# Projection and second norm cut into pieces, with their transposes between groups of qkv columns

## The chip, the cores and the metric

The kernel runs on one core of one Trainium2 chip. The metric is device time in microseconds of one execution; the time before is the median of three runs. Everything is fp32.

## The reference, cut to what matters

The input is x of 8 batches x 512 tokens x 576 features. First a rotation in a 64-dimensional subspace is applied per batch. Then one transformer block follows, with "attention" over the 16 heads of each token itself:

```
z = x @ U;  x = x + (z @ R - z) @ U.T                    # U from a QR, R = expm(skew(cond))
s1, c1, g1, s2, c2, g2 = split(silu(cond) @ ada_w + ada_b)
h = layernorm(x) * (1 + c1) + s1
q, k, v = h @ qkv_w + qkv_b                              # per token: 16 heads x 36
a = softmax(q k^T / 6) v                                 # 16 x 16 inside one token
x = x + g1 * (reorder(a) @ proj_w + proj_b)              # heads moved in front of tokens
h2 = layernorm(x) * (1 + c2) + s2
x = x + g2 * (gelu(h2 @ fc1_w + fc1_b) @ fc2_w + fc2_b)
```

The reordering in front of the projection mixes tokens: the attention result goes to device memory (`att_d`) and is read back in another layout (`at`).

## The kernel before, in words

After a preparation (QR, matrix exponential, modulation vectors) the kernel makes 16 passes, hb = 0 to 15. Each covers 256 tokens, two tiles (t = 0, 1) of 128; two passes make a batch (b = hb // 2). In pass hb the main loop does, in program order:

- `qkv(hb + 1, 0)`: the qkv product of tile 0 of the next pass. Its 1,728 columns are cut into four groups of 432; each group is five products over the feature chunks (`qkvp`, L631), one bank of PSUM, and a ScalarE copy to `qkv` (L638).
- `project(hb)`: for each tile, five transposes of `at` in two banks (`atr`, L702), two ScalarE copies to `aT` (L703), and two halves of the projection (`pj`, L709), which VectorE multiplies by the gate (`pt`, L711) and adds to `x1` (L712).
- `qkv(hb + 1, 1)`: the same for tile 1.
- `mlp_input(hb)`: the second layer norm of both tiles on VectorE (`normed`, L542 to L546, with one power on GpSimd, L545), then five pairs of transposes (`h2tr`, L555), each evicted by a ScalarE instruction that applies scale and shift (`h2T`, L558), and a GpSimd addition to `x1` of each tile (L721).
- `mlp(hb)`: 18 tiles f of fc1 (`fc`, L740; gelu on ScalarE, L742), and fc2 two tiles behind (L752). Weights are streamed from device memory through SP's queue in rings of four. In even passes the rotation of the next batch and its first norm (`gps` L577, `zps` L586, `rot` L594, `htr` L555) are put between the tiles of fc1.
- `attention(hb + 1)`: VectorE's products and reductions (`qk` L652, `sc` L658, `pv` L675, `att` L681), which run beside the MLP of pass hb, and the two stores to `att_d`.

The eight PSUM banks are three rings: `ps_mm` with two banks (tag "mm": qkvp, atr, pj, h2tr, and the rotation's products), `ps_f1` with two (tag "f1": fc1 alone), and `ps_acc` with four for fc2. A ring's next tile waits until the tile two before it has been evicted.

A scheduler orders each engine's instructions from the program order, the dependencies and its own durations. On the chip each engine follows its own list in that order. So an instruction late in the program can stand a little ahead of an earlier one that the scheduler believed to be waiting.

Of the kernel before, what the change touches and what calls it, by code (L numbers as in the profile page):

```python
# [9 lines left out]
F32 = mybir.dt.float32  # L10
U32 = mybir.dt.uint32
AF = mybir.ActivationFunctionType
ALU = mybir.AluOpType
# [4 lines left out]
B, S, D = 8, 512, 576  # L18
# [3 lines left out]
NT = S // 128  # L22
KROWS = [128, 128, 128, 128, 64]
NK = len(KROWS)
HALF = D // 2
# [4 lines left out]
TAU, M8 = 16, 8  # L30
# [12 lines left out]
def rotate_then_dit_block(  # L43
# [15 lines left out]
    nc = tc.nc  # L59
# [14 lines left out]
    xr_d = [dram.tile([NT, 128, D], F32, tag=f"xr_{b}", name=f"xr_{b}") for b in range(B)]  # L74
    att_d = [dram.tile([H, S, DH], F32, tag=f"att_{b}", name=f"att_{b}") for b in range(B)]

    ident = const.tile([128, 128], F32, tag="ident", name="ident")
# [9 lines left out]
    mod = const.tile([128, 4, NK, B], F32, tag="mod", name="mod")  # L87
# [3 lines left out]
    wproj = const.tile([128, NK, D], F32, tag="wproj", name="wproj")  # L91

    def srows(c):
        return 65 if c == 4 else 128
# [36 lines left out]
    with tc.manual_schedule(engines=engines), tc.tile_pool(name="prep", bufs=1) as prep, tc.tile_pool(name="qrs", bufs=2) as qrs, tc.tile_pool(  # L131
        name="ada", bufs=10
    ) as adap, tc.tile_pool(name="exs", bufs=1) as exs, tc.tile_pool(
        name="ps_qr", bufs=1, space=PSUM
    ) as ps_qr, tc.tile_pool(name="ps_a", bufs=1, space=PSUM) as ps_a, tc.tile_pool(
        name="ps_ex", bufs=2, space=PSUM
    ) as ps_ex, tc.tile_pool(name="ps_m", bufs=2, space=PSUM) as ps_m:
        m = prep.tile([128, NK, R], F32, tag="m", name="m")
# [260 lines left out]
        t = column_products(0)  # L399
        for j in range(R):  # L400
            t = qr_step(j, t)
# [11 lines left out]
        if True:  # L413
            sq = qrs.tile(wide(R), F32, tag="up0", name="sq", bufs=1)
            nc.vector.tensor_tensor(sq, m, m, ALU.mult)
            t = qrs.tile([128, R], F32, tag="t", name="t_sq")
# [42 lines left out]
            for c, rows in enumerate(KROWS):  # L459
                ps = ps_ex.tile([R, 128], F32, tag="ex", name=f"vt_{c}")  # L460
# [16 lines left out]
            ps = ps_m.tile([R, R], F32, tag="m", name="s_ps")  # L477
# [4 lines left out]
            for c, rows in enumerate(KROWS):  # L482
                ps = ps_m.tile([128, R], F32, tag="m", name=f"u_{c}")
# [5 lines left out]
            for n in range(2):  # L489
                ps = ps_m.tile([128, HALF], F32, tag="m", name=f"ut_{n}")  # L490
                nc.tensor.matmul(
                    ps,
                    lhsT=sneg.rearrange("p h i -> p (h i)"),
                    rhs=vt[:, n * HALF : (n + 1) * HALF],
                    start=True,
                    stop=True,
                )
                nc.scalar.copy(ut[:, n * HALF : (n + 1) * HALF], ps)
            for h in range(2):
                p = slice(h * R, (h + 1) * R)  # L500
# [3 lines left out]
    tiles = ctx.enter_context(tc.tile_pool(name="tiles", bufs=2))  # L504
    small = ctx.enter_context(tc.tile_pool(name="small", bufs=4))
    wst = ctx.enter_context(tc.tile_pool(name="wst", bufs=4))
    ps_mm = ctx.enter_context(tc.tile_pool(name="ps_mm", bufs=2, space=PSUM))
    ps_f1 = ctx.enter_context(tc.tile_pool(name="ps_f1", bufs=2, space=PSUM))
# [13 lines left out]
    ats = padded("at", 2)  # L522
    turn = {"xn": 0, "at": 0}

    def take(which, ring):
        turn[which] += 1
        return ring[(turn[which] - 1) % len(ring)]
# [7 lines left out]
    def normed(xt, name):  # L535

        st = small.tile([128, 2, 6], F32, tag="st", name=f"st_{name}")
        mv = small.tile([128, 2], F32, tag="mv", name=f"mv_{name}")
        rs = small.tile([128, 1], F32, tag="rstd", name=f"rstd_{name}")
        xn = take("xn", xns)  # L540
        for n in range(2):
            nc.vector.bn_stats(st[:, n, :], xt[:, n * HALF : (n + 1) * HALF])  # L542
        nc.vector.bn_aggr(mv, st)
        nc.vector.tensor_scalar(rs, mv[:, 1:2], LN_EPS, None, ALU.add)  # L544
        nc.gpsimd.tensor_tensor(rs, rs, mhalf[:, 0:1], ALU.pow)  # L545
        nc.vector.tensor_scalar(xn[:, 0:D], xt, mv[:, 0:1], rs, ALU.subtract, ALU.mult)  # L546
        return xn

    def modulated(dst_of, pair, shift, b, name):

        for c in range(NK):
            rows = srows(c)
            ps = ps_mm.tile([128, 2, 128], F32, tag="mm", name=f"{name}_{c}")
            for t in range(2):
                nc.tensor.transpose(ps[:, t, :], pair[t][:, c * 128 : (c + 1) * 128], ident)  # L555
            dst, src = dst_of(c, rows, ps[0:rows])
            sh, scl = mod[0:rows, shift, c, b : b + 1], mod[0:rows, shift + 1, c, b : b + 1]
            nc.scalar.activation(dst, src, AF.Identity, bias=sh, scale=scl)  # L558

    hTs = {}  # L560

    normed_x = {}
# [46 lines left out]
    def feature_major(b, half):  # L609

        if half == 0:
            hTs[b] = big.tile([128, NK, S], F32, tag="hT", name=f"hT_{b}")
        hT = hTs[b]

        def in_order(c, rows, ps):
            dst = hT[0:rows, c, :].rearrange("p (h t m) -> p t h m", t=NT, m=M8)[:, 2 * half : 2 * half + 2]
            return dst, ps.rearrange("p t (h m) -> p t h m", m=M8)

        modulated(in_order, normed_x.pop((b, half)), 0, b, f"htr_{b}_{half}")

    def qkv(hb, t):

        b, hT = hb // 2, hTs[hb // 2]
        i = 2 * (hb % 2) + t
        tok = tiles.tile([128, 3 * D], F32, tag="qkv", name=f"qkv_{b}_{i}", bufs=3)
        N = 3 * D // 4
        for n in range(4):
            ps = ps_mm.tile([128, N], F32, tag="mm", name=f"qkvp_{b}_{i}_{n}")
            for c in range(NK):
                k = srows(c)  # L630
                nc.tensor.matmul(  # L631
                    ps,
                    lhsT=hT[0:k, c, i * 128 : (i + 1) * 128],
                    rhs=wqkv[0:k, c, n * N : (n + 1) * N],
                    start=c == 0,
                    stop=c == NK - 1,
                )
            nc.scalar.copy(tok[:, n * N : (n + 1) * N], ps)  # L638
        return tok

    def attention(hb, toks):

# [42 lines left out]

    x1s = {}

    def project(hb, gate):
        b = hb // 2
        pair = []  # L690
        rows = att_d[b].rearrange("h (m t) d -> h m (t d)", t=TAU)
        for t in range(2):
            i = 2 * (hb % 2) + t
            at = take("at", ats)
            nc.sync.dma_start(out=at[:, 0:D], in_=rows[:, i * M8 : (i + 1) * M8, :])
            x1 = tiles.tile([128, D], F32, tag="x1", name=f"x1_{hb}_{t}", bufs=4)
            nc.sync.dma_start(out=x1, in_=xr_d[b][i])
            aT = tiles.tile([128, NK, 128], F32, tag="aT", name=f"aT_{hb}_{t}")
            for c0, c1 in ((0, 4), (4, 5)):
                ps = ps_mm.tile([128, 4, 128], F32, tag="mm", name=f"atr_{hb}_{t}_{c0}")  # L700
                for c in range(c0, c1):
                    nc.tensor.transpose(ps[:, c - c0, :], at[:, c * 128 : (c + 1) * 128], ident)  # L702
                nc.scalar.copy(aT[:, c0:c1, :], ps[:, 0 : c1 - c0, :])  # L703
            for n in range(2):
                cols = slice(n * HALF, (n + 1) * HALF)
                ps = ps_mm.tile([128, HALF], F32, tag="mm", name=f"pj_{hb}_{t}_{n}")
                for c in range(NK):
                    k = srows(c)
                    nc.tensor.matmul(ps, lhsT=aT[0:k, c, :], rhs=wproj[0:k, c, cols], start=c == 0, stop=c == NK - 1)  # L709
                tmp = tiles.tile([128, HALF], F32, tag="tmp", name=f"pt_{hb}_{t}_{n}", bufs=3)  # L710
                nc.vector.tensor_tensor(tmp, ps, gate[:, cols], ALU.mult)  # L711
                nc.vector.tensor_tensor(x1[:, cols], x1[:, cols], tmp, ALU.add)  # L712
            pair.append(x1)
        x1s[hb] = pair

    def mlp_input(hb, gb2):
        pair = [normed(x1, f"m{hb}_{t}") for t, x1 in enumerate(x1s[hb])]
        h2T = tiles.tile([128, NK, 256], F32, tag="h2T", name=f"h2T_{hb}")
        modulated(lambda c, rows, ps: (h2T[0:rows, c, :], ps.rearrange("p t s -> p (t s)")), pair, 2, hb // 2, f"h2tr_{hb}")
        for x1 in x1s[hb]:  # L720
            nc.gpsimd.tensor_tensor(x1, x1, gb2, ALU.add)  # L721
        return h2T

    LAG = 2

# [45 lines left out]
    NH = 2 * B  # L771
# [1 line left out]
        piece()  # L773
    feature_major(0, 0)
    feature_major(0, 1)
    toks = [qkv(0, 0), qkv(0, 1)]
    for v in (2, 3, 4, 5):
        for c in range(NK):
            load_ada(v, c, wst)
# [3 lines left out]
    for hb in range(NH):  # L783
        b = hb // 2
        aside = {}
        if hb % 2 == 0:
            gate_a, gate_m = gate_rows(0, b), gate_rows(1, b)
            gb2 = big.tile([128, D], F32, tag="gb2", name=f"gb2_{b}")
            nc.gpsimd.tensor_tensor(gb2, gate_m, b2, ALU.mult)
        if hb + 1 < NH:  # L790
            toks = [qkv(hb + 1, 0)]
        project(hb, gate_a)
        if hb + 1 < NH:
            toks.append(qkv(hb + 1, 1))
        if hb % 2 == 0 and b + 1 < B:
            aside = dict(zip((1, 3, 4, 6, 7, 8), rotation(b + 1)))
            aside |= {12: lambda: feature_major(b + 1, 0), 15: lambda: feature_major(b + 1, 1)}
        h2T = mlp_input(hb, gb2)
        mlp(hb, h2T, gate_m, aside)
        if hb + 1 < NH:  # L800
            attention(hb + 1, toks)
# [48 lines left out]
```

## Time and profile before

| | us |
|---|---|
| median of three runs (2331.64 to 2333.31) | 2332.75 |
| the profiled execution | 2331.75 |
| its span, first to last instruction | 2329.8 |
| TensorE products, busy | 2205.8 (95%) |
| TensorE weight loads, busy | 1656.0 (71%) |
| VectorE, busy | 1740.9 (75%) |
| ScalarE, busy | 385.3 (17%) |
| GpSimd, busy | 212.7 (9%) |
| DMA queue 1, share of 16 engines | 40.6% |

The mean granted TensorE clock is 0.986. A pass takes some 118 us where it is odd and 131 where it is even and carries the next batch's rotation; the whole of the 16 passes begins near 361 us. Busy time of products is modelled at its end, so it overstates how full TensorE is; the chain of waits tells more. Line numbers in the profile (L631) are those of the kernel printed above.

### The profile page before, as it was taken

To read this page: it belongs to the slowest core of one execution; us is meant where nothing else is said; L and a number is where in the kernel's file an instruction comes from. 1 tells how busy PE (TensorE), PEld (TensorE's weight loads), DVE (VectorE), ACT (ScalarE), POOL (GpSimd) and SP (SyncE) were. 2 spreads that over 40 slices of the span, in tenths; PEclk is the share of its full clock that TensorE was granted. 3 is DMA by queue.
4 is the path that set the end of the run, shared out by engine and by line. 5 is a ranking of instruction groups with operands and counts; after the bars stand their busy time and mean duration, and the time that the engine had idled before them with its cause. 6 is when DMAs were issued, how large, how long until landed. Compare 5 with 4: busy or idle time off the path is not lost.

```text
span 2329.8 us, 25839 instructions
## 1 busy us (share of the span) xinstructions
PE 2205.8 (95%) x9857; PEld 1656.0 (71%) x9857; DVE 1740.9 (75%) x2241; ACT 385.3 (17%) x872; POOL 212.7 (9%) x309
## 2 busy tenths in 40 slices
PE   6779788999999999999999999999999999999998
PEld 5668464767777676868686767777776868686877
DVE  8878399959595969768695959595968788595910
ACT  1012111211121202111111212121211112111110
POOL 2034001100010000010100010000100010101010
PEclk9999978999999999999999999999999999999999
DMA  7000322543536262626263444525262626252543
GB/s 251 1 4 2 115 74 62 162 135 102 143 108 189 60 178 57 201 63 165 69 197 100 126 113 150 147 84 160 95 180 65 171 67 165 75 157 82 152 121 111
DMA packets 206632, 271.41 MB, mean 116 GB/s; under 512 B 84115, under 2 KB 108395, under 8 KB 206510
## 3 DMA queue, kind: packets, MB, share of 16 engines
q1 hardware_dynamic: 206510, 269.77, 40.6%
q8 instruction: 79, 1.29, 0.2%
q14 instruction: 43, 0.35, 0.1%
HBM read 241.23 MB, written 28.35 MB: 116 GB/s over the span
## 4 chain that ended last, share of the span: by engine, by line
PE 89%; DVE 5%; ACT 2%; issue 1%; DMA 1%; POOL 1%; SPq 0%; POOLq 0%; ACTq 0%
PE fc L740 27%; PE fc L752 24%; PE qkvp L631 20%; PE pj L709 6%; PE zps L586 2%; PE dp L227 1%; PE rot L594 1%; PE h2tr L555 1%; PE htr L555 1%; PE aps L277 1%; ACT aT L703 1%; PE rp L219 1%; PE ada L118 1%; DVE up L257 1%; ACT qkv L638 1%
## 5 line engine op out<-in xcount | busy, mean ns | idle before, releaser
L740 PE MATMUL fc<-h2T,w 128*128 128x256 f32 (+1 forms) x2880 | 674.5, 380 | 0.0
L740 PEld LDWEIGHTS fc<-h2T,w 128*128 128x128 f32 (+1 forms) x2880 | 543.0, 191 | 83.2 <-issue 0.4
L752 PE MATMUL fc<-w,gt 128*128 128x288 f32 x2304 | 600.6, 405 | 0.0
L752 PEld LDWEIGHTS fc<-w,gt 128*128 128x128 f32 x2304 | 435.8, 189 | 109.6
L652 DVE TENSOR_TENSOR qk<-qkv 128x2304 f32<-128x2304 f32 x128 | 353.3, 2790 | 173.2 <-ACT qkv L638 173.2
L631 PE MATMUL qkvp<-wqkv,hT 128*128 128x432 f32 (+1 forms) x1280 | 474.6, 530 | 2.2 <-DVE pt L711 2.2
L631 PEld LDWEIGHTS qkvp<-wqkv,hT 128*128 128x128 f32 (+1 forms) x1280 | 244.2, 191 | 219.0 <-issue 212.4
L658 DVE TENSOR_REDUCE sc<-qk 128x64 f32<-128x2304 f32 x128 | 322.5, 2536 | 0.0
L675 DVE TENSOR_TENSOR pv<-sc,qkv 128x2304 f32<-128x2304 f32 x128 | 322.0, 2547 | 0.3
L681 DVE TENSOR_REDUCE att<-pv 128x144 f32<-128x2304 f32 x128 | 321.4, 2544 | 0.2
L764 DVE TENSOR_TENSOR mt<-fc,gate 128x288 f32<-128x288 f32 x64 | 29.3, 458 | 303.0 <-PE fc L752 283.3
L742 ACT ACTIVATE gt<-fc 128x256 f32<-128x256 f32 x288 | 110.4, 383 | 861.3 <-PE fc L740 861.1
L709 PE MATMUL pj<-wproj,aT 128*128 128x288 f32 (+1 forms) x640 | 163.9, 411 | 8.9 <-ACT aT L703 8.8
L638 ACT COPY qkv<-qkvp 128x432 f32<-128x432 f32 x128 | 66.3, 518 | 572.5 <-PE qkvp L631 572.5
L709 PEld LDWEIGHTS pj<-wproj,aT 128*128 128x128 f32 (+1 forms) x640 | 118.9, 190 | 45.6 <-ACT aT L703 15.1
L765 POOL TENSOR_TENSOR x<-x,mt 128x288 f32<-128x288 f32 x64 | 48.8, 795 | 949.3 <-DVE mt L764 949.3
L219 PE MATMUL rp<-m,ident 128*128 128x64 f32 (+42 forms) x128 | 40.7, 409 | 36.4 <-DVE m L265 32.6
L219 PEld LDWEIGHTS rp<-m,ident 128*128 128x128 f32 x128 | 32.0, 311 | 43.4 <-DVE m L265 38.2
L545 POOL TENSOR_TENSOR rstd_m<-rstd_m,mhalf 128x1 f32<-128x1 f32 x32 | 19.7, 616 | 458.9 <-DVE rstd_m L544 458.9
L545 POOL TENSOR_TENSOR rstd_a<-rstd_a,mhalf 128x1 f32<-128x1 f32 x32 | 25.3, 790 | 360.0 <-DVE rstd_a L544 360.0
L227 PE MATMUL dp<-t,ones 128*128 128x64 f32 (+42 forms) x128 | 39.0, 396 | 14.1 <-DVE sgs L235 13.6
L721 POOL TENSOR_TENSOR x<-x,gb 128x576 f32<-128x576 f32 x32 | 47.2, 1476 | 22.2 <-DVE xn L546 22.2
(204 smaller groups left out, 1402.0 us busy)
## 6 DMA issues: line engine op xcount, KB each, us to landing
w<-in_fc_w SPq DMA_DIRECT2D x288, 320.0 KB
w<-in_fc_w SPq DMA_DIRECT2D x288, 288.0 KB
xT<-in_x_t SPq DMA_DIRECT2D x16, 640.0 KB
xt<-in_x SPq DMA_DIRECT2D x32, 288.0 KB
xr<-xt SPq DMA_DIRECT2D x32, 288.0 KB
x<-xr SPq DMA_DIRECT2D x32, 288.0 KB
att<-att SPq DMA_DIRECT2D x32, 288.0 KB
at<-att SPq DMA_DIRECT2D x32, 288.0 KB
```

The costliest lines, as they stand in the source:

```text
L219: nc.tensor.matmul(rp[:, j:R], lhsT=ident[:, j : j + 1].to_broadcast([128, 128]), rhs=m[:, 0, j:R], start=True, stop=True,)
L227: nc.tensor.matmul(dp[:, j:R], lhsT=ones, rhs=t[:, j:R], start=True, stop=True)
L631: nc.tensor.matmul(ps, lhsT=hT[0:k, c, i * 128 : (i + 1) * 128], rhs=wqkv[0:k, c, n * N : (n + 1) * N], start=c == 0, stop=c == NK - 1,)
L638: nc.scalar.copy(tok[:, n * N : (n + 1) * N], ps)
L652: nc.vector.tensor_tensor(pr, q[:, c * HC : (c + 1) * HC].unsqueeze(2).to_broadcast([128, HC, H, DH]), k.unsqueeze(1).to_broadcast([128, H ...
L658: nc.vector.tensor_reduce(sc2[:, t, c * HC : (c + 1) * HC, :], pr, AX.X, ALU.add)
L675: nc.vector.tensor_tensor(pr, sc2[:, t, c * HC : (c + 1) * HC, :].unsqueeze(2).to_broadcast([128, HC, DH, H]), v.unsqueeze(1).to_broadcast ...
L681: nc.vector.tensor_reduce(att[:, c * HC : (c + 1) * HC, :], pr, AX.X, ALU.add)
L709: nc.tensor.matmul(ps, lhsT=aT[0:k, c, :], rhs=wproj[0:k, c, cols], start=c == 0, stop=c == NK - 1)
L740: nc.tensor.matmul(ps, lhsT=w1[0:k, c, :], rhs=h2T[0:k, c, :], start=c == 0, stop=c == NK - 1)
L742: nc.scalar.activation(gs[f], ps, AF.Gelu)
L752: nc.tensor.matmul(acc[t, n], lhsT=gs[f][:, t * 128 : (t + 1) * 128], rhs=w2[:, n * HALF : (n + 1) * HALF], start=f == 0, stop=f == NF - 1,)
```

## The change

`project` and `mlp_input` become a class `Projection` with four methods: `turn(t)` (the five transposes of attention tile t and their copies), `product(t, n)` (one half of the projection), `norm(t)` (the second norm of a tile, and the GpSimd addition to it), and `turn_normed(cs)` (the transposes and evictions of one or two feature chunks). `qkv` returns a function that does one group of columns. The main loop calls the pieces in a new order. The transposes of both kinds take their banks from `ps_f1` in place of `ps_mm`, and the second kind puts two feature chunks into one bank. The first norm's transposes keep their ring; their code is only written out in place. No instruction of arithmetic is added or removed.

```diff
-    def project(hb, gate):
-    def mlp_input(hb, gb2):
...
     def qkv(hb, t):
...
-        for n in range(4):
+        def group(n):
             ps = ps_mm.tile([128, N], F32, tag="mm", name=f"qkvp_{b}_{i}_{n}")
...
-        return tok
+        return tok, group
...
+    class Projection:
+        def __init__(self, hb, gate):
...
+            for t in range(2):
+                i = 2 * (hb % 2) + t
+                at = take("at", ats)
+                nc.sync.dma_start(out=at[:, 0:D], in_=rows[:, i * M8 : (i + 1) * M8, :])
+                x1 = tiles.tile([128, D], F32, tag="x1", name=f"x1_{hb}_{t}", bufs=4)
+                nc.sync.dma_start(out=x1, in_=xr_d[b][i])
...
+        def turn(self, t):
+            aT = tiles.tile([128, NK, 128], F32, tag="aT", name=f"aT_{self.hb}_{t}")
             for c0, c1 in ((0, 4), (4, 5)):
-                ps = ps_mm.tile([128, 4, 128], F32, tag="mm", name=f"atr_{hb}_{t}_{c0}")
+                ps = ps_f1.tile([128, 4, 128], F32, tag="f1", name=f"atr_{self.hb}_{t}_{c0}")
                 for c in range(c0, c1):
-                    nc.tensor.transpose(ps[:, c - c0, :], at[:, c * 128 : (c + 1) * 128], ident)
+                    nc.tensor.transpose(ps[:, c - c0, :], self.at[t][:, c * 128 : (c + 1) * 128], ident)
                 nc.scalar.copy(aT[:, c0:c1, :], ps[:, 0 : c1 - c0, :])
...
+        def product(self, t, n):
+            aT, x1 = self.aT[t], x1s[self.hb][t]
+            cols = slice(n * HALF, (n + 1) * HALF)
+            ps = ps_mm.tile([128, HALF], F32, tag="mm", name=f"pj_{self.hb}_{t}_{n}")
+            for c in range(NK):
+                k = srows(c)
+                nc.tensor.matmul(ps, lhsT=aT[0:k, c, :], rhs=wproj[0:k, c, cols], start=c == 0, stop=c == NK - 1)
+            tmp = tiles.tile([128, HALF], F32, tag="tmp", name=f"pt_{self.hb}_{t}_{n}", bufs=3)
+            nc.vector.tensor_tensor(tmp, ps, self.gate[:, cols], ALU.mult)
+            nc.vector.tensor_tensor(x1[:, cols], x1[:, cols], tmp, ALU.add)
+
+        def norm(self, t, gb2):
+            x1 = x1s[self.hb][t]
+            self.xn.append(normed(x1, f"m{self.hb}_{t}"))
             nc.gpsimd.tensor_tensor(x1, x1, gb2, ALU.add)
+
+        def turn_normed(self, cs):
...
+            ps = ps_f1.tile([128, 2, 2, 128], F32, tag="f1", name=f"h2tr_{self.hb}_{cs[0]}")
+            for k, c in enumerate(cs):
+                for t in range(2):
+                    nc.tensor.transpose(ps[:, k, t, :], self.xn[t][:, c * 128 : (c + 1) * 128], ident)
+            for k, c in enumerate(cs):
+                rows = srows(c)
+                nc.scalar.activation(
+                    self.h2T[0:rows, c, :],
+                    ps[0:rows, k].rearrange("p t s -> p (t s)"),
+                    AF.Identity,
+                    bias=mod[0:rows, 2, c, b : b + 1],
+                    scale=mod[0:rows, 3, c, b : b + 1],
+                )
...
-        if hb + 1 < NH:
-            toks = [qkv(hb + 1, 0)]
-        project(hb, gate_a)
-        if hb + 1 < NH:
-            toks.append(qkv(hb + 1, 1))
+        pr = Projection(hb, gate_a)
+        (tok0, q0), (tok1, q1) = [qkv(hb + 1, t) if hb + 1 < NH else (None, lambda n: None) for t in range(2)]
+        toks = [tok0, tok1]
+        for n in range(3):
+            q0(n)
+        pr.turn(0)
+        q0(3)
+        pr.product(0, 0)
+        pr.turn(1)
+        pr.product(0, 1)
+        pr.norm(0, gb2)
+        pr.product(1, 0)
+        pr.product(1, 1)
+        pr.norm(1, gb2)
+        for n in range(3):
+            q1(n)
+        pr.turn_normed((0, 1))
+        q1(3)
+        pr.turn_normed((2, 3))
+        pr.turn_normed((4,))
+        h2T = pr.h2T
...
-        h2T = mlp_input(hb, gb2)
         mlp(hb, h2T, gate_m, aside)
```

More of the change, by code (lines that the diff above doesn't have):

```diff
@@ L547, in normed @@
         return xn
[L549 to L558, printed above, removed]
     hTs = {}
@@ L613, in feature_major @@
         hT = hTs[b]
[L615 to L619, printed above, removed]
+        pair = normed_x.pop((b, half))
+        for c in range(NK):
+            rows = srows(c)
+            ps = ps_mm.tile([128, 2, 128], F32, tag="mm", name=f"htr_{b}_{half}_{c}")
+            for t in range(2):
+                nc.tensor.transpose(ps[:, t, :], pair[t][:, c * 128 : (c + 1) * 128], ident)
+            nc.scalar.activation(
+                hT[0:rows, c, :].rearrange("p (h t m) -> p t h m", t=NT, m=M8)[:, 2 * half : 2 * half + 2],
+                ps[0:rows].rearrange("p t (h m) -> p t h m", m=M8),
+                AF.Identity,
+                bias=mod[0:rows, 0, c, b : b + 1],
+                scale=mod[0:rows, 1, c, b : b + 1],
+            )
     def qkv(hb, t):
@@ L686, in rotate_then_dit_block @@
     x1s = {}
-    def project(hb, gate):
[L689 to L698, printed above, removed]
+    class Projection:
+        def __init__(self, hb, gate):
+            self.hb, self.gate, b = hb, gate, hb // 2
+            rows = att_d[b].rearrange("h (m t) d -> h m (t d)", t=TAU)
+            self.at, self.aT, self.xn, x1s[hb] = [], [], [], []
+            for t in range(2):
[4 more added lines that the diff above has]
+                nc.sync.dma_start(out=x1, in_=xr_d[b][i])
+                self.at.append(at)
+                x1s[hb].append(x1)
+        def turn(self, t):
+            aT = tiles.tile([128, NK, 128], F32, tag="aT", name=f"aT_{self.hb}_{t}")
@@ L699, in project @@
             for c0, c1 in ((0, 4), (4, 5)):
-                ps = ps_mm.tile([128, 4, 128], F32, tag="mm", name=f"atr_{hb}_{t}_{c0}")
+                ps = ps_f1.tile([128, 4, 128], F32, tag="f1", name=f"atr_{self.hb}_{t}_{c0}")
                 for c in range(c0, c1):
-                    nc.tensor.transpose(ps[:, c - c0, :], at[:, c * 128 : (c + 1) * 128], ident)
+                    nc.tensor.transpose(ps[:, c - c0, :], self.at[t][:, c * 128 : (c + 1) * 128], ident)
                 nc.scalar.copy(aT[:, c0:c1, :], ps[:, 0 : c1 - c0, :])
[L704 to L712, printed above, removed]
@@ L713, in project @@
-            pair.append(x1)
-        x1s[hb] = pair
-    def mlp_input(hb, gb2):
[L717 to L722, printed above, removed]
+            self.aT.append(aT)
+        def product(self, t, n):
+            aT, x1 = self.aT[t], x1s[self.hb][t]
+            cols = slice(n * HALF, (n + 1) * HALF)
+            ps = ps_mm.tile([128, HALF], F32, tag="mm", name=f"pj_{self.hb}_{t}_{n}")
+            for c in range(NK):
+                k = srows(c)
[3 more added lines that the diff above has]
+            nc.vector.tensor_tensor(x1[:, cols], x1[:, cols], tmp, ALU.add)
@@ new lines, in norm @@
+        def norm(self, t, gb2):
+            x1 = x1s[self.hb][t]
+            self.xn.append(normed(x1, f"m{self.hb}_{t}"))
+            nc.gpsimd.tensor_tensor(x1, x1, gb2, ALU.add)
+        def turn_normed(self, cs):
+            if cs[0] == 0:
+                self.h2T = tiles.tile([128, NK, 256], F32, tag="h2T", name=f"h2T_{self.hb}")
+            b = self.hb // 2
+            ps = ps_f1.tile([128, 2, 2, 128], F32, tag="f1", name=f"h2tr_{self.hb}_{cs[0]}")
+            for k, c in enumerate(cs):
+                for t in range(2):
+                    nc.tensor.transpose(ps[:, k, t, :], self.xn[t][:, c * 128 : (c + 1) * 128], ident)
+            for k, c in enumerate(cs):
+                rows = srows(c)
+                nc.scalar.activation(
+                    self.h2T[0:rows, c, :],
+                    ps[0:rows, k].rearrange("p t s -> p (t s)"),
+                    AF.Identity,
+                    bias=mod[0:rows, 2, c, b : b + 1],
+                    scale=mod[0:rows, 3, c, b : b + 1],
+                )
@@ L775, in rotate_then_dit_block @@
     feature_major(0, 1)
-    toks = [qkv(0, 0), qkv(0, 1)]
+    toks = []
+    for t in range(2):
+        tok, group = qkv(0, t)
+        for n in range(4):
+            group(n)
+        toks.append(tok)
     for v in (2, 3, 4, 5):
```

## The prediction

> **What bounds the kernel now.** I read the chain of waits first, because one engine's busy share is an average over stages with different limits. It says that TensorE carries nearly all of the span:
>
> ```profile
> PE 89%; DVE 5%; ACT 2%; issue 1%; DMA 1%; POOL 1%; SPq 0%; POOLq 0%; ACTq 0%
> ```
>
> So the question is where this engine's queue stands still. The chain in order of time (start, duration, what) shows it, here for pass hb = 6, which begins at 1115.33 us:
>
> ```profile
> 1115.33 14.53 PE qkvp L631 x40
> 1129.85 0.02 issue
> 1129.88 0.52 ACT qkv L638
> 1130.39 0.52 ACT aT L703
> 1130.91 0.04 issue
> 1130.96 5.12 PE pj L709 x20
> 1136.08 0.45 PE atr L702 x4
> ...
> 1137.88 5.12 PE pj L709 x20
> 1143.00 14.53 PE qkvp L631 x40
> 1157.53 0.02 issue
> 1157.55 0.53 ACT qkv L638
> 1158.08 0.04 issue
> 1158.13 0.44 PE h2tr L555 x2
> ...
> 1160.13 1.73 PE fc L740 x8
> ```
>
> An fp32 product is two instructions, so x40 is four column groups of five products; the prices in this stream are 14.53 / 4 = 3.63 us for a qkv group, 5.12 / 2 = 2.56 for a projection half, 2.16 for an fc1 tile (rows "PE fc L740 x10"), and 0.11 for a transpose that waits for nothing (the htr rows inside the MLP: 0.44 for four). Where transposes stand, the chain leaves TensorE for ScalarE's evictions. In such a pass it takes:
> - from 1129.86 to 1130.96, 1.10 us for five transposes worth 0.55: 0.55 lost;
> - from 1136.08 to 1137.88, 1.80 for five more: 1.25 lost;
> - from 1157.53 to the end of the first fc1 tile at 1161.86, 4.33 for ten transposes and that tile (1.10 + 2.16): 1.07 lost.
>
> That is **about 2.85 us per pass**. The odd pass at 997.12 loses the same: 46.53 us from its start to its first fc1 tile's end, against 43.68 of work (29.06 + 10.24 + 2.20 + 2.16 and rounding). An even pass loses 0.26 more where the next batch's z product waits for its bank (zps 2.42 us against 2.16 elsewhere).
>
> Then I read VectorE's timeline, since it makes the normalised rows that the second transposes need (start, duration, groups, idle before):
>
> ```profile
> 1126.80 5.03 DVE L652 TENSOR_TENSOR qk<-qkv 128x2304 f32<-128x2304 f32 x2 [10.91 <-ACT qkv L638]
> 1146.62 3.61 DVE L652 TENSOR_TENSOR qk<-qkv 128x2304 f32<-128x2304 f32 x1
> 1153.54 0.58 DVE L546 TENSOR_SCALAR xn<-x,mv_m,rstd_m 128x576 f32<-128x576 f32 x1 [0.66 <-POOL rstd_m L545]
> 395.85 0.45 DVE L712 TENSOR_TENSOR x<-x,pt 128x288 f32<-128x288 f32 x1
> 396.01 1.55 POOL L721 TENSOR_TENSOR x<-x,gb 128x576 f32<-128x576 f32 x1 [0.69 <-DVE xn L546]
> ```
>
> VectorE is full from 1126.80, when three qkv groups are out, until the second normalised tile ends at 1154.12. Today the transposes want that tile at 1157.5. This is the second runner.
>
> **What the Trainium skill says.** "PSUM — Partial Sum Buffer", section "Engine vs sequencer instructions", states that matmuls start and complete in program order and the other engines' queues are strict FIFO. The trace agrees: 20 projection instructions stand behind a 0.59 us eviction at 1136.55. So a transpose placed between groups costs 0.11 only if its input and bank are ready. The same page, section "PSUM bank collisions raise a hardware error", says that two engines must not be on one bank and quadrant together; thus an eviction waits for the whole bank, and a pair of transposes in one bank is released by its second eviction. "SBUF — State Buffer", section "Who interferes with whom", says that VectorE and GpSimd share a port pair which whoever issues first holds for the whole instruction, a two-input VectorE add included. The trace shows both sides: the qk product at 1146.62 began behind GpSimd's add (1146.41, 1.40 us) and took 3.61 against 2.54; the short add at 395.85 began 0.16 us ahead of GpSimd's, kept its 0.45, and GpSimd's took 1.55.
>
> **The change, part by part, on pass 6's clock.** The instruction counts are equal; the order and banks change. I took the order from the built program and the durations from the rows above.
>
> TensorE: q0's first three groups end at 1126.23. Five transposes of the first attention tile go to fc1's banks, free since the last gelu: 1126.79. q0's fourth group: 1130.42. Their copies (0.52 and 0.27 us) lie under that group. First projection half: 1132.98; five transposes of tile 1: 1133.54; three halves: 1136.10, 1138.66, 1141.22. The halves use the two other banks, freed by VectorE's pt. It reaches them at 1134.20 and 1137.39 and ends 0.37 later, ahead of the needs at 1136.10 and 1138.66. Then q1's three groups: 1152.12; one transpose of xn tile 0; one product of q1's fourth group, which the scheduler slipped in: 1152.95. There TensorE wants **xn tile 1**.
>
> VectorE, from 1126.80 in its new order: two qk 4.94, reduction 2.46, pt 0.37, reduction 2.46, x 0.36, pt 0.37, stats 0.37, x 0.36 = 1138.49; 0.19 wait for the third half; pt, stats, x, aggregate 1.22; qk 2.46; rstd0 starts 1142.36, and xn0 starts 0.81 later as at 1152.73 to 1153.54 today (0.37 of it filled by pt): 1143.17; xn0 0.50, x 0.36, stats 0.74, reduction 2.46, aggregate 0.12, qk 2.46, rstd 0.06, reduction 2.46, xn1 0.58 = **1152.91**. So the tile comes when it is wanted; I charge 0.10. GpSimd's add starts about 0.08 after that short x add, so I take the 395.85 case: no delay. If it holds the port first, xn1 slips by up to 1.07 (3.61 - 2.54). A gain below zero delay is excluded, as TensorE cannot use an earlier tile.
>
> After it: three transposes 0.33, four products 2.90 (1156.3), four transposes 0.44, two more 0.22: 1156.95. fc1's first tile needs the bank of the pair (2, 3), released at 1157.94: q1's copy 0.52, two evictions 0.53 each. In even passes the scheduler fills this with the two gps products (1.11), in odd ones with two products of the following pass's q0 (1.45): nothing lost. Pass 14 has neither: 0.99 lost.
>
> Sum against the profiled execution: 7 odd passes (1 to 13) x 2.75 = 19.2; 6 even (2 to 12) x (2.85 + 0.26 - 0.10) = 18.1; pass 14, 2.85 - 0.10 - 0.99 = 1.8. Pass 15 has no qkv to hide under; its second attention transposes lose a copy's wait (about 0.65) and the fc1 entry some 0.6: 1.3. Pass 0: q0's fourth group now stands behind at0's transposes, whose load issues at 366.8, long before 375; the second half is paced by VectorE, where pt of tile 1 comes at 395.0 against 394.8 today, and xn1 at 408.4; adding the work behind gives 418.6 against 419.5 for the same work: 0.9. **Total 41.3 us.** The profiled execution took 2331.75 (span 2329.8 plus 1.95 around it): 2290.5. The median of the runs is 1.0 above it: **2291.5**.
>
> Costed at nothing: attention's loads. The second at load issues at 1106.93, and its transposes now stand at 1133, earlier by 4.4 than today, still 26 us later. SP's order changes only by a neighbour or two (an attention store behind one w1 issue, 0.33 us); VectorE idles 13.2 us before the MLP's end, of which 2.8 goes. GpSimd's two adds are the same and come 0 to 4 us earlier. The qkv bank that an odd pass holds through its MLP is wanted by nobody there.
>
> **Rivals.**
> 1. *GpSimd's add takes the port first.* For: 3.61 us at 1146.62. Against: 395.85. xn1 is 1.07 late in 14 passes: 15 us back, **2306.5**.
> 2. *VectorE becomes the bound and the kernel slower*: xn1 late by more than 2.95 us (2.85 plus the charged 0.10) eats each pass's gain, because q1's last products stand behind it. Price: were the rstd power blocked by a qk product as at 392.57 (2.74 us against 0.55) and the add too, 2.2 + 1.1 = 3.3 late: 14 x 0.4 = 5 lost, **2337**. Against: pt and a reduction, not qk, follow rstd in the new order.
> 3. *The change gives nothing here* because the removed waits reappear as bank waits in fc1's ring (fc1's first tile behind two evictions in every pass, xn1 late too): 2.85 back, **2332**. Against: the fillers gps and q0 are in the built order.
>
> **How the numbers follow.** The forecast has 0.68, rival 1 and mixtures 0.26, rival 2 0.04, rival 3 0.02. Even full removal of every listed wait, all 14 of the 0.10, pass 14's 0.99 and pass 0's two bank waits included (1.25 and 2.23, of which 0.9 is counted), gives 41.3 + 1.4 + 1.0 + 2.6 = 46.3: 2286.5. So the range runs from 2286 to 2308, past rival 1. What a measurement here can tell from no change is 0.2%, 4.7 us. Faster 0.94, same 0.02, slower 0.04.
>
> **What would show it.** Right: in the chain the copies of aT vanish, projection and qkv rows follow each other with 0.55 of transposes between, and h2tr stands within q1's fourth group; the first fc1 tile of an odd pass ends near 45.2 us after the start, 1.45 of the next pass included. Wrong: "DVE xn" in the chain before h2tr with 1 us or more per pass, qk or x rows stretched by a GpSimd add, or pj waiting for pt.

## The result and the profile after

The changed kernel takes **2293.2 us** (median of six runs, 2290.71 to 2298.73); the kernel before, beside it, 2331.69 (six runs, 2330.76 to 2333.31). The ratio is 0.9836, with an interval of 0.9823 to 0.9849: 38.5 us faster, where 41 had been forecast.

The profiled execution of the changed kernel is its longest run, 2298.73. Against a second profile of the same kernel (span 2292.6) it lost 4.1 us ahead of pass 0's first attention transpose (380.83 against 376.71), most of it where loads of the modulation weights were waited for. Therefore the passes are compared by their lengths, not by their clock times. The second profile has the same passes: from pass 1's first attention transpose to pass 15's it took 1681.03 us, against 1681.06 here.

From the start of one pass's block of `qkvp` products ahead of the attention transposes to the start of the next pass's, the odd and the even pass are these:

| us | odd pass | even pass | two passes | two passes, gain |
|---|---|---|---|---|
| before | 118.21 | 130.86 | 249.06 | |
| after | 116.85 | 126.48 | 243.34 | 5.73 |

An odd pass of the changed kernel also holds 1.45 us of the next one's first group. So it gained 2.81 net and the even pass 2.92; the forecast had 2.75 and 3.01.

TensorE's timeline of an odd pass of the changed kernel, hb = 5, shows where this comes from (start, duration, operation, form, instructions, idle before and its releaser):

```profile
990.72 11.05 PE L630 MATMUL qkvp<-wqkv,hT 128*128 128x432 f32 x30
1001.61 0.71 PE L709 MATMUL atr<-ident,at 128*128 128x128 f32 x5
1002.16 3.79 PE L630 MATMUL qkvp<-wqkv,hT 128*128 128x432 f32 x10
1005.79 2.59 PE L719 MATMUL pj<-wproj,aT 128*128 128x288 f32 x10
1008.22 0.71 PE L709 MATMUL atr<-ident,at 128*128 128x128 f32 x5
1008.76 7.45 PE L719 MATMUL pj<-wproj,aT 128*128 128x288 f32 x30
1016.05 11.05 PE L630 MATMUL qkvp<-wqkv,hT 128*128 128x432 f32 x30
1026.94 0.27 PE L737 MATMUL h2tr<-ident,xn 128*128 128x128 f32 x1
1027.05 0.89 PE L630 MATMUL qkvp<-wqkv,hT 128*128 128x432 f32 x2
1028.35 0.55 PE L737 MATMUL h2tr<-ident,xn 128*128 128x128 f32 x3 [0.41 <-DVE xn L546]
```

From the first attention transpose at 1001.61 to the second tile's qkv at 1016.05 there is no idle entry. Take the fourth group, 3.63, out of these 14.44 us and 10.81 are left for ten transposes and four projection halves. Before, the same work took from 1129.86 to 1143.00 in the rows of the prediction, 13.14 us. So **2.33 us per pass are gained at the projection**. The rest, some 0.5, is gained at the entry of fc1, where one idle entry is left: the second normalised tile.

The head of the chain of waits on the changed kernel's page has moved:

```profile
PE 71%; DVE 15%; issue 8%; DMA 3%; POOL 2%; ACT 1%; SPq 0%; POOLq 0%; DVEq 0%; ACTq 0%
```

TensorE's share of the chain fell from 89% to 71%. TensorE is as busy as before (95% of the span on both pages), and it waits less. The chain follows each wait to what released it. In passes 1 to 14 a wait for the second normalised tile is left, and it leads into VectorE. The end of this detour in the chain's own rows for pass 6 of the changed kernel (start, duration, what):

```profile
1140.63 2.52 DVE sc L658
1143.15 0.50 DVE xn L546
1143.65 0.04 issue
1143.69 0.55 PE h2tr L737 x3
1144.24 2.90 PE qkvp L630 x8
```

The wait is half a microsecond, but behind it the chain stays off TensorE for as far back as the other engines' work is joined up: from 1001.79 to 1028.35 in pass 5, and from 1106.30 to 1143.69 in pass 6. So the percentages name the second runner, not the price: the price is the wait itself.

The timelines of VectorE and GpSimd in that pass answer the question of the port pair:

```profile
1134.39 0.45 DVE L722 TENSOR_TENSOR x<-x,pt 128x288 f32<-128x288 f32 x1
1143.56 6.23 DVE L652 TENSOR_TENSOR qk<-qkv 128x2304 f32<-128x2304 f32 x2
1134.56 1.55 POOL L727 TENSOR_TENSOR x<-x,gb 128x576 f32<-128x576 f32 x1 [0.69 <-DVE xn L546]
1143.72 3.65 POOL L727 TENSOR_TENSOR x<-x,gb 128x576 f32<-128x576 f32 x1 [2.46 <-DVE xn L546]
```

VectorE's short add began 0.17 us ahead of GpSimd's and kept its 0.45. GpSimd's second addition began behind a qk product and took 3.65. On the page its mean went from 1476 ns to 2525, while that of VectorE's qk products fell from 2790 to 2680:

```profile
L719 PE MATMUL pj<-wproj,aT 128*128 128x288 f32 (+1 forms) x640 | 160.9, 406 | 1.1 <-ACT aT L710 1.1
L727 POOL TENSOR_TENSOR x<-x,gb 128x576 f32<-128x576 f32 x32 | 80.8, 2525 | 46.5 <-DVE xn L546 46.5
```

No wait for GpSimd's additions shows there. The first row has a part of the main gain: the idle time ahead of the projection's products was 8.9 us before and is 1.1 now, all of it in passes 0 and 15. The waits ahead of the transposes, which are gone too, are not in this row.

### The profile page after: what moved, and what is told of

It reads as the page before. It is cut to its first block, busy times and chain, and to the rows that moved or that the text cites. A ratio compares the mean times of both kernels' runs of the same rounds, so it can differ in the third digit from the quotient of the medians.

```text
span 2297.0 us, 25890 instructions
## 1 busy us (share of the span) xinstructions
PE 2188.7 (95%) x9857; PEld 1656.7 (72%) x9857; DVE 1728.4 (75%) x2241; ACT 381.0 (17%) x872; POOL 251.5 (11%) x309
## 4 chain that ended last, share of the span: by engine, by line
PE 71%; DVE 15%; issue 8%; DMA 3%; POOL 2%; ACT 1%; SPq 0%; POOLq 0%; DVEq 0%; ACTq 0%
PE fc L764 27%; PE fc L776 24%; PE qkvp L630 8%; DVE qk L652 4%; DVE sc L658 4%; PE zps L575 2%; DMA gate<-gates_d 1%; PE rot L583 1%; PE dp L227 1%; PE htr L609 1%; PE aps L277 1%; DMA aw<-in_ada_w 1%; PE rp L219 1%; DVE xn L546 1%; PE h2tr L737 1%
## 5 line engine op out<-in xcount | busy, mean ns | idle before, releaser
L630 PE MATMUL qkvp<-wqkv,hT 128*128 128x432 f32 (+1 forms) x1280 | 484.5, 532 | 3.9 <-DVE pt L721 3.9
L652 DVE TENSOR_TENSOR qk<-qkv 128x2304 f32<-128x2304 f32 x128 | 339.2, 2680 | 159.3 <-ACT qkv L637 159.3
L727 POOL TENSOR_TENSOR x<-x,gb 128x576 f32<-128x576 f32 x32 | 80.8, 2525 | 46.5 <-DVE xn L546 46.5
L545 POOL TENSOR_TENSOR rstd_a<-rstd_a,mhalf 128x1 f32<-128x1 f32 x32 | 32.9, 1027 | 352.6 <-DVE rstd_a L544 352.6
```

The source lines that it names most:

```text
L630: nc.tensor.matmul(ps, lhsT=hT[0:k, c, i * 128 : (i + 1) * 128], rhs=wqkv[0:k, c, n * N : (n + 1) * N], start=c == 0, stop=c == NK - 1,)
L652: nc.vector.tensor_tensor(pr, q[:, c * HC : (c + 1) * HC].unsqueeze(2).to_broadcast([128, HC, H, DH]), k.unsqueeze(1).to_broadcast([128, H ...
```

## The experiments

Theory: the gain is TensorE's stalls, and it needs both halves of the edit, an order that puts independent work behind each group of transposes and banks that are free at that moment. Rivals: the banks alone do it, the order alone does it, or VectorE, which runs level with TensorE in the new order, bounds the pass. The runs of before beside the first four kernels had a median of 2334.19 (16 runs), beside the others 2334.89 (9 runs). All results in one table, two passes measured as above:

| kernel | median us | ratio to before, interval | two passes |
|---|---|---|---|
| the change, run again | 2293.93 | 0.9826 (0.9813 to 0.984) | 243.33 |
| new banks, old order | 2313.68 | 0.9911 (0.9896 to 0.9925) | 245.97 |
| new order, old banks | 2333.19 | 0.9997 (0.9988 to 1.0005) | 248.77 |
| projection's half alone | 2301.76 | 0.9858 (0.9843 to 0.9872) | 244.37 |
| second norm's half alone | 2326.06 | 0.9964 (0.995 to 0.9979) | 247.75 |
| fourth group cut in two | 2287.08 | 0.9799 (0.9786 to 0.9812) | 242.14 |
| the same, and pass 15 mended | 2286.9 | 0.9796 (0.9782 to 0.9809) | 242.14 |
| second tile's norm 2.2 us later | 2301.45 | 0.9859 (0.9846 to 0.9873) | 243.62 |

### The new banks in the old order

```diff
-        for n in range(3):
+        for n in range(4):
             q0(n)
         pr.turn(0)
-        q0(3)
         pr.product(0, 0)
-        pr.turn(1)
         pr.product(0, 1)
-        pr.norm(0, gb2)
+        pr.turn(1)
         pr.product(1, 0)
         pr.product(1, 1)
-        pr.norm(1, gb2)
-        for n in range(3):
+        for n in range(4):
             q1(n)
+        pr.norm(0, gb2)
+        pr.norm(1, gb2)
         pr.turn_normed((0, 1))
-        q1(3)
```

> The order of before (all four qkv groups, then the projection of both tiles, then the other four groups, then the second norm and its transposes), but the new banks: both kinds of transposes in fc1's ring, two feature chunks to a bank. Theory (the order hides ScalarE's evictions, the banks only make it possible): the first eviction still stands bare (0.55 us lost in a pass), the second loses its bank wait but keeps a copy (about 0.6 of 1.25), the fc1 entry is filled by the next pass's qkv products or by gps (about 0.3 left of 1.07), so about 1.4 us gained in a pass: near 2311 us. Rival (banks alone are the gain): 2293 us. Rival (banks do nothing without the order): 2332 us.

Measured: 2313.68, near the expectation of 2311; the two passes gained 3.09 of the 5.73. TensorE's timeline of its pass 5:

```profile
1009.41 0.71 PE L709 MATMUL atr<-ident,at 128*128 128x128 f32 x5
1010.69 5.12 PE L719 MATMUL pj<-wproj,aT 128*128 128x288 f32 x20 [0.56 <-ACT aT L710]
```

The five transposes now go without a bank wait, but the products behind them still wait for the copies, 0.56 us here and 0.57 for the second tile. The stretch takes 12.47 us (1009.41 to 1021.88), 0.67 less than before and 1.66 more than after. The banks alone are half the gain, and more of that half lies behind this stretch than in it (3.09 against 2 x 0.67).

### The new order with the old banks

```diff
-                ps = ps_f1.tile([128, 4, 128], F32, tag="f1", ...)
+                ps = ps_mm.tile([128, 4, 128], F32, tag="mm", ...)
...
-            ps = ps_f1.tile([128, 2, 2, 128], F32, tag="f1", ...)
+            ps = ps_mm.tile([128, 2, 2, 128], F32, tag="mm", ...)
```

> The new order with the old banks: both kinds of transposes in the ring of qkv and projection products, two feature chunks to a bank. Theory: TensorE then waits inside the new order for banks: about 0.6 us at q0's fourth group behind the first copies, about 0.75 at the second tile's last transpose behind VectorE's pt, about 1 us for the second normalised tile; 0.5 to 1 us gained in a pass: near 2321 us. Rival (the order alone is the gain): 2293 us.

Measured: 2333.19, no gain that the time shows, and 0.29 us of two passes; a part of the gain had been expected, near 2321. TensorE's timeline of its pass 5:

```profile
1014.87 3.89 PE L630 MATMUL qkvp<-wqkv,hT 128*128 128x432 f32 x10 [0.18 <-ACT aT L710]
1022.31 0.33 PE L709 MATMUL atr<-ident,at 128*128 128x128 f32 x1 [0.68 <-ACT aT L710]
1033.95 7.52 PE L630 MATMUL qkvp<-wqkv,hT 128*128 128x432 f32 x20 [0.40 <-DVE pt L721]
1042.28 0.55 PE L737 MATMUL h2tr<-ident,xn 128*128 128x128 f32 x3 [0.70 <-DVE xn L546]
```

In a ring of two banks, every tile waits for the tile two before it. With the transposes in that ring, the group placed behind them waits for the transposes' own copy, the next transposes do too, and a qkv group now waits for VectorE's `pt`. The work that was to hide the copies stands behind them instead. So order and banks are not two gains that add: the order is worth next to nothing without the banks, and about 20 us with them (2313.68 to 2293.93). This kernel also issues the loads of the attention tiles where the change has them and puts two chunks into a bank, so neither of these is a gain of its own.

### Each half alone

The projection's half: the second norm goes back to one chunk per bank of `ps_mm`, behind all four groups.

```diff
-            ps = ps_f1.tile([128, 2, 2, 128], F32, tag="f1", ...)
+            ps = ps_mm.tile([128, 2, 2, 128], F32, tag="mm", ...)
...
-        for n in range(3):
+        for n in range(4):
             q1(n)
-        pr.turn_normed((0, 1))
-        q1(3)
-        pr.turn_normed((2, 3))
-        pr.turn_normed((4,))
+        pr.norm(0, gb2)
+        pr.norm(1, gb2)
+        for c in range(NK):
+            pr.turn_normed((c,))
```

> Only the first half of the change: the attention transposes between qkv groups and products in fc1's banks; the second norm, its transposes and their banks as before, after all eight qkv groups. Theory: the first two gaps go (0.55 + 1.25 us in a pass, and some 0.25 more since a projection half that doesn't wait takes 2.43 us in the trace and not 2.56), the third (1.07 us) stays: about 2.0 us gained in a pass, near 2303 us. Rival (VectorE's second tile is the real limit): the gain turns into a wait for it before the second transposes, 2315 us or more.

Measured: 2301.76, where 2303 had been expected; 4.69 of two passes, 2.35 per pass. This is the 2.33 read off the projection's stretch.

The second norm's half: the attention transposes go back to `ps_mm`, all four groups of q0 stand ahead of them, and both norms stand behind the projection.

```diff
-                ps = ps_f1.tile([128, 4, 128], F32, tag="f1", ...)
+                ps = ps_mm.tile([128, 4, 128], F32, tag="mm", ...)
...
-        for n in range(3):
+        for n in range(4):
             q0(n)
         pr.turn(0)
-        q0(3)
         pr.product(0, 0)
-        pr.turn(1)
         pr.product(0, 1)
-        pr.norm(0, gb2)
+        pr.turn(1)
         pr.product(1, 0)
         pr.product(1, 1)
+        pr.norm(0, gb2)
```

> Only the second half of the change: qkv groups and projection ordered as before with the old banks for the attention transposes; the second norm's transposes among the last qkv groups, in fc1's banks. Theory: the third gap (1.07 us) goes, and the second normalised tile is late by 0.2 us or so, since TensorE comes later here: about 0.9 us gained in a pass, near 2319 us, and the two halves add up to the whole (38 us). Rival (the tile from VectorE is the limit): no gain here, 2330 us.

Measured: 2326.06, 7 us slower than expected; 1.31 of two passes, 0.65 per pass. Here the halves do add, nearly: 4.69 + 1.31 = 6.00 against 5.73 for the whole. The projection's half is four fifths of the gain, and the second norm's half is worth two thirds of the 0.97 that the prediction had for it.

### One wait taken away: the fourth group cut in two

If the wait for the second normalised tile is what is left, the transposes should stand two products later, within the fourth group. `group` gets a range of chunks for this:

```diff
         for n in range(3):
             q1(n)
+        q1(3, 0, 2)
         pr.turn_normed((0, 1))
-        q1(3)
+        q1(3, 2, NK)
         pr.turn_normed((2, 3))
```

> The changed kernel with one edit: the first transposes of the second norm stand after two products of q1's fourth group by the program, both tiles together, where the scheduler had put the first tile's transpose before that group and the second tile's after one product. Theory (TensorE waits 0.35 to 0.41 us in a pass for VectorE's second normalised tile): the need moves later by 0.6 to 0.7 us, the wait goes, two passes take 242.6 us in place of 243.34 and the kernel 5 us less, near 2288 us. Rival (the modelled wait is no real one, or it comes back at the banks of fc1's ring): no change, 2293 us.

Measured: 2287.08, where 2288 had been expected; two passes 242.14, 1.2 less than the change beside it. TensorE's timeline of its pass 5 has no wait:

```profile
1012.38 12.50 PE L634 MATMUL qkvp<-wqkv,hT 128*128 128x432 f32 x34
1024.72 0.60 PE L742 MATMUL h2tr<-ident,xn 128*128 128x128 f32 x4
1025.16 2.34 PE L634 MATMUL qkvp<-wqkv,hT 128*128 128x432 f32 x6
```

VectorE's tile comes at 1024.63 there, 0.09 us ahead of its need. The head of the chain of waits on this kernel's page is TensorE's again:

```profile
PE 91%; DVE 5%; DMA 1%; issue 1%; POOL 1%; ACT 1%; SPq 0%; POOLq 0%; ACTq 0%; DVEq 0%
```

So the 71% above came from that one wait in each pass. From pass 1's first attention transpose to pass 15's this kernel took 1672.66 us against 1681.03: 8.37, or 0.60 for each of 14 passes.

### Pass 15 mended as well

```diff
-            nc.gpsimd.tensor_tensor(x1, x1, gb2, ALU.add)
+            if not self.last:
+                nc.gpsimd.tensor_tensor(x1, x1, gb2, ALU.add)
...
+        q1(3, 0, 2)
+        pr.turn_normed((0,) if pr.last else (0, 1))
+        q1(3, 2, NK)
+        for cs in ((1,), (2,), (3,), (4,)) if pr.last else ((2, 3), (4,)):
+            pr.turn_normed(cs)
+        if pr.last:
+            for x1 in x1s[hb]:
+                nc.gpsimd.tensor_tensor(x1, x1, gb2, ALU.add)
```

In the last pass `turn_normed` also takes its banks from `ps_mm`.

> The edit before, and in pass 15, which has no qkv products to hide under, the second norm's transposes in single chunks in the idle ring of the products, as the kernel before had them, and GpSimd's two additions after both norms. Theory (pass 15 lost 0.9 us by bank waits, 0.79 + 0.22, and by GpSimd's add holding VectorE's x add for 1.40 us in place of 0.45): pass 15 up to its first fc2 product takes 25.6 to 26.2 us in place of 27.28, and the kernel 6 to 7 us less than the changed one, near 2286.5 us. Rival (pass 15 is slow by TensorE's clock after the idle time alone, mean 0.87 there): 27 us stays.

Measured: 2286.9 (five runs, 2283.98 to 2288.04), not to be told from the kernel above by its time. By its trace, pass 15 takes 25.83 us from its first attention transpose to its first fc2 product, within the expected range, against 26.94 in the kernel above, 27.28 in the change and 26.99 in the change's second profile. That it fell in the range is in part luck: one of the two causes behind the range did not take place, and TensorE's clock had a share in the gain (see pass 15 below). The move of GpSimd's addition did nothing. The scheduler still issued it right after the first tile's norm, as VectorE's timeline shows:

```profile
2193.28 1.40 DVE L728 TENSOR_TENSOR x<-x,pt 128x288 f32<-128x288 f32 x1
```

This version and the one above are the quickest that were run, about 7 us below the change.

### The second tile's norm made later

To see how hard VectorE holds TensorE, the second tile's statistics are computed four times (the same values): six instructions more, 2.2 us.

```diff
-            nc.vector.bn_stats(st[:, n, :], ...)
+            for _ in range(4 if name[0] == "m" and name[-1] == "1" else 1):
+                nc.vector.bn_stats(st[:, n, :], ...)
```

> The changed kernel with the statistics of the second tile's second norm computed four times over, the same values: six more VectorE instructions of 0.37 us, 2.2 us in the way of the second normalised tile in each pass. In the built order the scheduler lets four products of q1's fourth group pass the second tile's transpose, in place of one. Theory: those three more products (2.18 us) hide it; about 0.3 us more in a pass at the fc1 entry, as the evictions start later: near 2297 us. Rival (the tile's delay is paid in full, as my slower case had it): 14 x 2.2 = 31 us more, 2324 us.

Measured: 2301.45, 7.5 more than the change, between the two expectations and much nearer to the theory's. Two passes grew by 0.29 alone. TensorE's timeline of its pass 5 tells why:

```profile
1026.51 3.06 PE L631 MATMUL qkvp<-wqkv,hT 128*128 128x432 f32 x8
1029.97 0.55 PE L738 MATMUL h2tr<-ident,xn 128*128 128x128 f32 x3 [0.40 <-DVE xn L547]
```

The scheduler let four products of the fourth group pass, where it had let one, and the wait kept its 0.4. In the two profiles (spans 2301.0 and 2292.6, 8.4 apart) passes 1 to 14 have 2.3 of the difference, pass 15, which has nothing to fill with, 3.3, and the stretch up to pass 1 2.8. Of these 2.8, 2.4 lie ahead of pass 0's first transposes, where the edit has not acted yet. And in pass 15 not all is waiting: the granted clock is 0.50 there for 10.24 us, against 6.83 in the change.

## Why the prediction was right, and which of its terms were not

The mechanism held. The waits for the copies of aT are gone from passes 1 to 14, the second transposes stand within the fourth group, and fc1's entry is filled with gps or q0 products, in pass 14 alone with nothing, as forecast. That the total came so near, 38.5 against 41, is in part luck, since terms that were off cancel. By its own steps:

- **0.55 + 1.25 at the projection, measured 2.33.** The sum priced a half at 2.56 us, from rows of 5.12 for two. Such a row begins after a wait: from its first instruction's start to the second's it is 0.35 us, to the later ones' 0.24 (1130.96, 1131.30, 1131.55), and its modelled end, 1136.08, lies 0.16 behind the start of the transposes that follow. In the stream a half takes 2.43 (1005.79 to 1008.22, and a third of 7.29). Four halves at 0.13 make the missing 0.52.
- **0.10 for xn tile 1, measured 0.57 in the odd pass and 0.50 in the even.** These are the starts of the transposes against the end of the work ahead: 1027.05 + 0.73 = 1027.78 and 1028.35. VectorE did as forecast: 25.87 us from its first qk product to the end of xn1, forecast 26.11. But TensorE, on cheaper halves, wanted the tile half a microsecond sooner. The one wrong price moved both terms, and they cancel to 0.1: 2.75 against 2.81.
- **2.75 + 0.26 in even passes, measured 2.92.** The 0.26 was read as the z product's wait for its bank. In the new order a tile of fc1 follows gps instead, and its first two starts are 0.19 late in the same way, though its bank had been free since 1148.64 and it began at 1148.85. So at most 0.07 of the 0.26 was the bank; what the rest is, no run shows.
- **Pass 14: 1.8, measured 1.70** (118.20 to 115.05, with 1.45 of the next pass's work brought in). The 0.99 bank wait was real: fc1 began at 2122.05, 1.05 us behind the end of the transposes' work.
- **Pass 0: 0.9, measured 0.2** (from its first attention transpose to pass 1's, 134.33 us before, 134.10 and 134.09 in the two profiles after). In the first of these TensorE waits 3.87 us for `pt` ahead of q1. In the second it waits 2.81 us for the load of the second attention tile instead, which the forecast costed at nothing, and the length is the same. So what TensorE saved in front went into another wait; that VectorE paces this pass fits both, but no edit tried it.
- **Pass 15: +1.3, measured -0.87**, the term with the wrong sign (26.41 us to the first fc2 product before, 27.28 after).

TensorE's, GpSimd's and VectorE's timelines of pass 15 of the changed kernel show the last one:

```profile
2211.53 0.87 PE L737 MATMUL h2tr<-ident,xn 128*128 128x128 f32 x6 [3.52 <-DVE xn L546]
2213.19 0.69 PE L737 MATMUL h2tr<-ident,xn 128*128 128x128 f32 x2 [0.79 <-ACT h2T L740]
2214.10 9.33 PE L764 MATMUL fc<-h2T,w 128*128 128x256 f32 x30 [0.22 <-ACT h2T L740]
2206.24 1.40 POOL L727 TENSOR_TENSOR x<-x,gb 128x576 f32<-128x576 f32 x1 [0.69 <-DVE xn L546]
2206.57 1.40 DVE L722 TENSOR_TENSOR x<-x,pt 128x288 f32<-128x288 f32 x1
```

Up to the end of the projection it gained 0.83 (forecast 0.65). Then it lost 0.52 at GpSimd's addition to the first tile. Before, VectorE's short add, held back by the projection, began 1.02 us behind GpSimd's (2240.34 and 2239.32), took 0.69, and VectorE was idle again before the last half came. Now it began 0.33 us behind and took 1.40, so that the last half's `pt` began 0.74 us behind the start of what TensorE did after that half (2208.37 and 2207.63), against 0.20 before (2242.28 and 2242.08). The edit that aimed at this addition did not move it, so this part is read from the traces alone.

And it lost 1.18 from the second transposes to the first fc2 product. Two things differ there. With two chunks to a bank and two banks, TensorE waits for whole pairs of evictions, with no qkv product to fill. And every profile has a stretch near this place in which the granted clock is 0.50, and the five compared here have it at different points (all in us; "idle" is what the rows show ahead of transposes and fc1):

| kernel | second transposes begin | clock 0.50 | of this behind that begin | idle | to the first fc2 product |
|---|---|---|---|---|---|
| before | 2245.46 | 2244.34 to 2251.16 | 5.70 | 0.44 | 10.56 |
| the change | 2211.53 | 2212.53 to 2219.36 | 6.83 | 1.01 | 11.74 |
| the change, second profile | 2207.37 | 2207.81 to 2214.64 | 6.83 | 0.71 | 11.46 |
| fourth group cut in two | 2201.85 | 2201.82 to 2208.65 | 6.80 | 0.69 | 11.41 |
| pass 15 mended | 2198.24 | 2196.58 to 2203.41 | 5.17 | 0.44 | 10.29 |

At 0.50 an fc1 product instruction takes 0.427 us from start to start, behind it 0.216. So a microsecond more of the slow clock under work costs half a microsecond. An estimate from this: of the 1.18, 1.13 x 0.5 = 0.56 is the clock, and the rest, about 0.6, is left for the waits. The kernel with pass 15 mended and the kernel before check it, since they have the same waits: 0.53 x 0.5 = 0.27, and they differ by 0.27. By the same estimate the mended pass owes 0.83 of its 1.45 against the change to the clock, and about 0.6 to the banks. What decides where the slow stretch begins was not tried.

All terms together: passes 1 to 13 gained 37.1 (forecast 37.3), and pass 1 to the end 38.0 (forecast 40.4). The difference of 2.4 is pass 15's 2.2 and small change.

The rivals: the first, GpSimd's add ahead at the port, came true in pass 15 alone. There the short add grew by 0.95 and the pass lost 0.52; in the other passes VectorE was ahead by 0.17. The second, VectorE as the bound, is half true: TensorE does wait for VectorE in every pass, by 0.5, but far from the 2.95 at which the gain would be gone, and 2.2 us of delay cost only 7.5 in all, since qkv products pass the transposes. The third, waits that reappear at the banks, is what the new order does in the old ring (2333.19 measured there), and in fc1's ring it appears in passes 14 and 15.

One reading of the prediction is weaker than it says. It saw TensorE's program order in 20 projection instructions behind an eviction, but these read the evicted tile themselves. The changed kernel shows the order better: eight qkv instructions at 1144.08, whose inputs and bank had been in use since 1142.46, stood behind three transposes that waited for VectorE.

## What to carry to other kernels

Work placed behind a producer hides the producer's latency only if the two use different buffers: ask of each moved piece which ring its output takes, and what released the slot two before. Price an instruction from start to start in a full stream, not from a row that follows a wait; a wrong price moves the demand time as well as the cost, and a race between two engines that is won by 0.1 us on paper is open. And look at the last pass on its own: what hides a wait everywhere else is missing there, and after a wait the granted clock belongs in the comparison.

## What the runs showed of the hardware that was not expected

- The idle time shown ahead of a TensorE row is too small, since the ends of its rows are modelled: 0.41 shown in pass 5 of the change, 0.57 from the end of the work ahead, counted from starts, to the start of the transpose. Taking the wait away brought 0.60 per pass.
- At the port pair it decides who begins first, even by a sixth of a microsecond. VectorE's short add took 0.45 when it began 0.17 us ahead of GpSimd's, and 1.40 when it began 0.33 behind; GpSimd's took 1.55 behind the short add and 3.65 behind a qk product. This agrees with "SBUF — State Buffer", section "Who interferes with whom", of the Trainium skill.
- TensorE's granted clock was 0.50 for 6.83 us in pass 15 of nine of the ten profiles and for 10.24 in the one with the later norm, and 1.00 all through passes 1 to 14. So the mended pass 15 was ahead of the unmended ones by 1.1 to 1.45 us, depending on the profile that it is compared with.
